# Layer 1's keys, values, contexts and queries of the first batch, made in steps beside the Mamba scans of the second batch

## The chip, the cores and the metric

The kernel runs on one core of one Trainium2 chip. A core has TensorE (PE: matmuls, with weight loads shown apart as PEld), VectorE (DVE), ScalarE (ACT), GpSimd (POOL) and SyncE (SP, which here issues nearly all transfers). The metric is device time in microseconds (us). The kernel before took 5376.03 us, the median of three runs (5373.67 to 5379.39).

## The reference

Four layers work on an image batch `x` of 2 x 256 channels x 48 x 48, all in fp32. In the kernel, L = 48 * 48 = 2304 tokens per batch.

```python
# layer 0: two Mamba branches, forward and backward over the tokens
xs = silu(conv1d(xi)); dt = softplus(...); Bm, Cm = ...
h = exp(d_t * A) * h + (d_t * u_t) * B_t      # 512 channels x 16 states, over 2304 tokens
y = sum_n(h * C_t) + u * D
x = x + (y_f + y_b) @ out_proj_w.T

# layer 1, on v = group-normalized x (32 groups of 8 channels, over a whole image)
q, k, v = relu(t @ Wq + bq) * scale, relu(t @ Wk + bk), t @ Wv + bv
ctx = einsum('bhnd,bhne->bhde', k, v)         # 8 heads of 32, a sum over ALL tokens of a batch
out = einsum('bhnd,bhde->bhne', q, ctx)
img = depthwise_conv3x3(out) + dw_b
t = repbn(t + img @ Wproj + bproj)
t = repbn(t + gelu(t @ Wfc1 + bfc1) @ Wfc2 + bfc2)
x = x + t

# layers 2 and 3: attention, a graph layer with experts (edge_index sorted by target),
# attention again, and a mixture of experts; not touched here
```

Two things matter: the group normalization needs the statistics of a whole image, and the contexts `ctx` need the keys and values of all tokens of that image before its first output can be made. Batch 0's image is finished halfway through layer 0.

## The kernel before, in words

Channels lie on the 128 partitions (256 channels are two halves, `k` or `m`), tokens along the free axis. The residual `E.xres` stays in SBUF. A *piece* is W = 384 tokens; each batch has NCH = 6 pieces, NTB = 18 blocks of 128 tokens.

**Layer 0** (`layer0`) runs 24 *scan steps*, the list `order`: batch 0 forward (steps 0 to 5), batch 0 backward (6 to 11), batch 1 forward (12 to 17), batch 1 backward (18 to 23), one piece each. A scan step (`scan`) handles 4 channel blocks x 16 states: for each, ScalarE makes `hs` (L454, an exponential into one of five PSUM banks), VectorE runs the recurrence (L460 or L463) and, for 40 of 64, the product with `cc` (L468); GpSimd does the other 24 of these products and all of `db` (L437). TensorE sums the products `hc` into `yp` with the identity (`add_state`, L422). Each of the two kinds of `hc` has four buffers. SyncE loads `bb` and `cc` for each group of four states (L432, L434), two buffers each.

A scan step has 32 *slots* (one per two states). The list `beside` holds generators that are advanced as slots go by, each written (steps, number of steps, slot by which to be done): `prepare` for the next scan step, `project_out` for the last piece of a backward step, and either `project_in` (steps 0 to 9) or three steps of `head_products` (steps 10 to 21). In step 13 the statistics of batch 0 are taken beside the scan (`group_stats`: twelve `bn_stats`, then two small matmuls with `gmat` and a square root). While scans run, all products of the beside work go through one PSUM bank, the tag `mm` of pool `ps` (`hold`), so a product waits until the one before it has been read. `head_products` has 12 rounds of three steps: load six blocks `w_eo`; a product `pg` read into `part`; twelve tiny products `pu` read into `ub`.

**Layer 1** (`layer1`), for b = 0 and then 1: group-normalize the batch into `E.xn` (`group_norm`, L597); a loop over 18 blocks makes keys and values `kv` (L611, bias L616, ReLU L617) and sums the contexts `cx` (L619), masked per head with `hmask`; then six pieces go through `image` (queries L633, times contexts L640, written to the padded image `img`), `conv` (18 taps on VectorE, L655 and L659), `project` (L670) and `mlp` (L691 and L710). The image is three pieces ahead. `group_norm(1)`, with the statistics of batch 1, is called after the fourth piece of batch 0. After each piece come lists of the edge sort for layer 2 (`sort_list`, L902 to L925), which nothing in layer 1 reads.

The order in which the program is written is a priority: the framework's planner orders each engine's instructions by it and by its own estimate of when they are ready, so an instruction from later in the text may be put into a gap. The semaphores follow from the data. Each engine then runs its queue strictly in that order.

## Time and profile before

One execution was profiled. It took 5420.46 us, with a span of 5418.6 us from its first to its last instruction; the three timed runs had a median of 5376.03 us.

| stretch of the profile | from, to (us) | what |
|---|---|---|
| start of layer 0 | 0 to 103.9 | first projections, first `prepare` |
| scan steps, batch 0 | 103.9 to 1286.0 | 12 steps of 89.2 to 104.3 us |
| scan steps, batch 1 | 1286.0 to 2431.6 | 12 steps of 89.7 to 102.5 us, the last one 87.9 with the end of layer 0 |
| layer 1 | 2431.6 to 3131.9 | 700.3 us |
| layers 2 and 3, output | 3131.9 to 5418.6 | not touched |

Over the span PE is busy 88%, DVE 65%, ACT 44% and POOL 44%. A busy share counts the time in which an engine has an instruction in it. PE's ends are modelled: back to back, a matmul instruction of 128x384 takes a step of 0.32 us, though it is shown with 0.49 us, since neighbours overlap; one fp32 product is two such instructions. The granted clock is the share of full speed at which TensorE was allowed to run (mean 0.954). In the view of waits, "A <- B" means that an idle time of A's engine ended when B was done.

### The profile page before, as it was taken

The page shows a single profiled execution, that of the slowest core. Times are in us where ns is not written, and L with a number is a line of the kernel's source. Part 1 is how long each engine was busy: PE and PEld are TensorE (multiplying, and loading weights), DVE is VectorE, ACT ScalarE, POOL GpSimd, SP SyncE. Part 2 cuts the span into 40 slices and gives each one's busy share as a digit, 9 for nine tenths or more (in the row PEclk, how much of TensorE's full clock was granted, in tenths as well). Part 3 has the DMA queues.
Part 4 walks back from the last instruction along what each step waited for, and adds up shares of the span by engine and source line. Part 5 has one row for each costly group of instructions (what it writes and reads, how often), then busy time and mean ns, then how long its engine had stood idle before and what let it go on. Part 6 is the DMA issues. An engine that isn't in the chain of part 4 may idle for free. (4 is left out here: it accounts for less than half of the span.)

```text
span 5418.6 us, 47326 instructions
## 1 busy us (share of the span) xinstructions
PE 4773.2 (88%) x15246; PEld 2642.9 (49%) x15246; DVE 3503.3 (65%) x5372; ACT 2370.0 (44%) x4939; POOL 2403.7 (44%) x1308
## 2 busy tenths in 40 slices
PE   7888888888787778879999989999799999999897
PEld 3444444444343344435555555556455455555675
DVE  4999888898999888899996244546534401212343
ACT  5767767666677666642223223422122222222111
POOL 2888888788888888880000000038502100000331
PEclk8999999999899899989999999999898999999899
DMA  4454454444454444431110000111121200000422
GB/s 152 166 177 173 164 178 170 159 162 151 160 174 158 173 166 158 148 137 61 33 45 6 1 16 0 40 29 30 15 72 52 61 7 9 6 9 6 83 83 94
DMA packets 185425, 499.13 MB, mean 92 GB/s; under 512 B 33382, under 2 KB 106474, under 8 KB 184906
## 3 DMA queue, kind: packets, MB, share of 16 engines
q1 hardware_dynamic: 176458, 483.23, 26.1%
q0 software_dynamic: 8704, 12.73, 1.6%
q8 instruction: 124, 2.03, 0.2%
q14 instruction: 139, 1.14, 0.1%
HBM read 422.73 MB, written 73.15 MB: 92 GB/s over the span
## 5 line engine op out<-in xcount | busy, mean ns | idle before, releaser
L422 PE MATMUL yp<-hc,ident 128*128 128x384 f32 x3072 | 1201.7, 523 | 253.2 <-DVE hc L468 210.9
L437 POOL TENSOR_TENSOR db<-dtu,bb 128x1536 f32<-128x1536 f32 x384 | 1329.1, 3462 | 64.6 <-DVE hs L463 21.0
L422 PEld LDWEIGHTS yp<-hc,ident 128*128 128x128 f32 x3072 | 576.2, 199 | 830.2 <-DVE hc L468 408.5
L468 POOL TENSOR_TENSOR hc<-ho,cc 128x384 f32<-128x384 f32 x576 | 584.9, 1023 | 189.9 <-DVE ho L460 82.6
L468 DVE TENSOR_TENSOR hc<-hs,cc 128x384 f32<-128x384 f32 x960 | 496.7, 537 | 57.9 <-PE yp L422 56.6
L454 ACT ACTIVATE hs<-dt,negab 128x384 f32<-128x384 f32 x768 | 435.9, 581 | 93.9 <-DVE hc L468 43.1
L454 ACT ACTIVATE hs<-dt,negaf 128x384 f32<-128x384 f32 x768 | 433.7, 581 | 65.0 <-DVE ho L460 28.8
L463 DVE TENSOR_TENSOR_SCAN hs<-hs,state,db 128x384 f32<-128x384 f32 x400 | 393.8, 1006 | 50.2 <-POOL db L437 23.8
L460 DVE TENSOR_TENSOR_SCAN hs<-hs,state,db 128x384 f32<-128x384 f32 x400 | 395.3, 1007 | 27.4 <-POOL db L437 19.6
L1813 POOL DMA_INDIRECT xe<-xt_d,token x48 | 47.4, 988 | 754.4 <-issue 715.3
L302 PE MATMUL mm<-xw,w_cv 128*128 128x384 f32 x768 | 292.4, 520 | 60.2 <-DVE xres L364 22.0
L1748 PE MATMUL po<-at,xtok 128*128 128x384 f32 x864 | 329.7, 506 | 8.2 <-ACT at L1746 8.1
L953 POOL PARTITION_ALL_REDUCE most<-most x1 | 0.4, 381 | 721.4 <-DVE mx L811 721.4
L1739 PE MATMUL sp<-qT,xn 128*128 128x384 f32 x864 | 317.2, 486 | 0.0
L1746 ACT ACTIVATE at<-sp 128x384 f32<-128x384 f32 x216 | 104.8, 491 | 473.1 <-PE sp L1739 473.0
L1395 PE MATMUL ph<-xn,w 128*128 128x384 f32 x768 | 287.0, 515 | 16.8 <-DMA y_d<-y 5.9
L1399 ACT ACTIVATE hid<-ph,vec 128x384 f32<-128x384 f32 x192 | 110.6, 581 | 337.2 <-PE ph L1395 244.6
L691 PE MATMUL pf<-t,wfc 128*128 128x384 f32 x768 | 255.3, 488 | 0.0
L710 PE MATMUL po<-hid,wfc 128*128 128x384 f32 x768 | 253.6, 486 | 0.0
L470 ACT COPY state<-hs 128x1 f32<-128x1 f32 x800 | 117.7, 155 | 293.6 <-DVE hc L468 291.7
L463 DVE TENSOR_TENSOR_SCAN ho<-hs,state,db 128x384 f32<-128x384 f32 x240 | 238.9, 995 | 10.3 <-ACT hs L454 10.2
L460 DVE TENSOR_TENSOR_SCAN ho<-hs,state,db 128x384 f32<-128x384 f32 x240 | 238.6, 994 | 7.0 <-ACT hs L454 6.6
(442 smaller groups left out, 7970.5 us busy)
## 6 DMA issues: line engine op xcount, KB each, us to landing
bb<-bcd SPq DMA_DIRECT2D x192, 768.0 KB
cc<-bcd SPq DMA_DIRECT2D x192, 768.0 KB
xw<-xi_d SPq DMA_DIRECT2D x24, 774.0 KB
w<-in_m_w SPq DMA_DIRECT2D x16, 1024.0 KB
y_d<-y SPq DMA_DIRECT2D x32, 384.0 KB
ye<-y_d SPq DMA_DIRECT2D x32, 384.0 KB
xi_d<-xz SPq DMA_DIRECT2D x48, 192.0 KB
z_d<-xz SPq DMA_DIRECT2D x48, 192.0 KB
```

The lines of the kernel that those rows point to most:

```text
L302: nc.tensor.matmul(px, lhsT=w_cv[b, s][:, d * 4 + k, :], rhs=xw[:, d, o : o + W], start=k == 0, stop=k == 3,)
L422: nc.tensor.matmul(yp[d], lhsT=E.ident, rhs=hc, start=False, stop=summed[d] == NS)
L437: nc.gpsimd.tensor_tensor(db, bc(dtu[:, d, :], [P, GN, W], 1), bb, ALU.mult)
L454: nc.scalar.activation(hs, dt[:, d, :], AF.Exp, scale=nega[s][:, d * NS + n : d * NS + n + 1])
L460: nc.vector.tensor_tensor_scan(to, hs, db[:, j], init, ALU.mult, ALU.add)
L463: nc.vector.tensor_tensor_scan(to[:, ::-1], hs[:, ::-1], db[:, j, ::-1], init, ALU.mult, ALU.add)
L468: (nc.gpsimd if on_pool else nc.vector).tensor_tensor(hc, to, cc[:, j, :], ALU.mult)
L691: nc.tensor.matmul(pf, lhsT=wfc1[:, k, f * P : (f + 1) * P], rhs=t1[:, k, :], start=k == 0, stop=k == 1,)
L710: nc.tensor.matmul(po[m], lhsT=wfc2[:, f, m * P : (m + 1) * P], rhs=hid[:, i, :], start=f == 0, stop=f == 15,)
L1395: nc.tensor.matmul(ph, lhsT=w1[:, e, k, f * P : (f + 1) * P], rhs=xn[:, k, c * W : (c + 1) * W], start=k == 0, stop=k == 1,)
L1739: nc.tensor.matmul(sp, lhsT=xn[:, k, t0 + i * P : t0 + (i + 1) * P], rhs=qT[:, k, c * W : (c + 1) * W], start=k == 0, stop=k == 1,)
L1748: nc.tensor.matmul(po[m], lhsT=xtok[:, i, m * P : (m + 1) * P], rhs=at, start=i == 0, stop=i == MT - 1,)
```

## The change

Batch 0's part of layer 1 that precedes the convolution moves into layer 0, and batch 1's statistics move too.

- `contexts`, a new generator, is chained behind `head_products`. It loads `Wqkv` into the space of `w_in`, and makes for each piece of batch 0 the normalized tokens (ScalarE), keys and values of three blocks (biases by a matmul of one row) and their sum `cx`; then, for each piece again, the queries and their product with the masked contexts, `qc`, stored to DRAM (`qc_d`). It has 61 steps, which take their SBUF from tiles of `project_in`.
- The chained generators are advanced eight steps in each of the scan steps 10 to 22 (`n_late` = 97 / 13, rounded up), where it was three steps in 10 to 21.
- `piece_stats` takes the two `bn_stats` of each finished piece right behind its `project_out`, for both batches; `group_stats` keeps only the rest. Batch 0's is still in step 13; batch 1's is now at the start of layer 1.
- Layer 1 starts with batch 1: its statistics, its keys and values. Normalizing either batch goes on by pieces between the blocks of that loop. Batch 0's image is filled by `fetch`: a load of `qc` by SyncE, and two copies on GpSimd. Batch 1 keeps its image by matmuls, now called `second`. The loads of `Wfc1` and `Wfc2` come behind the first three `fetch`es.
- `hmask` is built at the start of the program.

```diff
+            self.hmask = const.tile([P, P], F32, name="hmask")
+            same_block(self, wp, self.hmask, 5, 32**-0.5)
...
+def piece_stats(E, b, c):
+    for k in range(2):
+        at = b * L + c * W
+        E.nc.vector.bn_stats(E.st[:, b, k, c, :], E.xres[:, k, at : at + W])
+        yield
...
     for k in range(2):
-        st = wp.tile([P, NCH, 6], F32, tag="st", name="st")
-        for c in range(NCH):
-            nc.vector.bn_stats(st[:, c, :], xb[:, k, c * W : (c + 1) * W])
-            yield
-        nc.vector.bn_aggr(mv[:, k, :], st)
+        nc.vector.bn_aggr(mv[:, k, :], E.st[:, b, k])
...
+    def contexts():
...
+        nc.sync.dma_start(wqkv, p["Wqkv"].rearrange("(k p) m -> p k m", p=P))
+        nc.sync.dma_start(bkv, p["bqkv"][C:].unsqueeze(0))
...
+        def normed(c):
+            xn = up.tile([P, 2, W], F32, tag="pos", name="xn0")
+            for k in range(2):
+                nc.scalar.activation(
+                    xn[:, k, :], E.xres[:, k, c * W : (c + 1) * W], AF.Identity,
+                    bias=off[:, k : k + 1], scale=E.gn[:, 0, 1, k : k + 1],
+                )
+            return xn
+
+        for c in range(NCH):
+            xn = normed(c)
+            yield
...
+            for t in range(3):
+                pk = ps.tile([P, 2 * C], F32, tag="mm", name="pk")
+                for k in range(2):
+                    nc.tensor.matmul(
+                        pk, lhsT=xn[:, k, t * P : (t + 1) * P], rhs=wqkv[:, k, C:],
+                        start=k == 0, stop=False,
+                    )
+                nc.tensor.matmul(pk, lhsT=E.mean_c[0:1, :], rhs=bkv, start=False, stop=True)
+                nc.scalar.activation(kv[t][0], pk[:, :C], AF.Relu)
+                nc.scalar.copy(kv[t][1], pk[:, C:])
+                yield
+            pc = ps.tile([P, C], F32, tag="mm", name="pc")
+            for m in range(2):
+                ms = slice(m * P, (m + 1) * P)
+                for t in range(3):
+                    nc.tensor.matmul(
+                        pc[:, ms], lhsT=kv[t][0][:, ms], rhs=kv[t][1][:, ms], start=t == 0, stop=t == 2
+                    )
+            if c == 0:
+                nc.scalar.copy(cx, pc)
+            else:
+                nc.vector.tensor_tensor(cx, cx, pc, ALU.add)
+            yield
...
+        for c in range(NCH):
+            xn = normed(c)
+            yield
...
+            for m in range(2):
+                pq = hold()
+                for k in range(2):
+                    nc.tensor.matmul(
+                        pq, lhsT=wqkv[:, k, m * P : (m + 1) * P], rhs=xn[:, k, :],
+                        start=k == 0, stop=k == 1,
+                    )
+                nc.scalar.activation(q[:, m, :], pq, AF.Relu, bias=E.v("bq", m, 1))
+                yield
...
+            for m in range(2):
+                pi = hold()
+                nc.tensor.matmul(pi, lhsT=cx[:, m, :], rhs=q[:, m, :], start=True, stop=True)
+                nc.scalar.copy(qc[:, m, :], pi)
+                if m:
+                    nc.sync.dma_start(E.qc_d[:, c], qc)
+                yield
...
-    heads = head_products()
+    heads = chain(head_products(), contexts())
+    n_late = -(-(36 + 1 + 2 * 5 * NCH) // (len(order) - 1 - len(pieces)))
...
-        beside = [(after, 2, 5)] if after else []
+        beside = [(after, 4, 8)] if after else []
...
-        elif i < len(pieces) + 12:
-            beside.append((islice(heads, 3), 3, 32))
+        elif len(pieces) <= i < len(order) - 1:
+            beside.append((islice(heads, n_late), n_late, 32))
         if (b, s, step) == (1, "f", 1):
-            beside.append((group_stats(E, up, lambda: hold()[:, 0:2], 0), 15, 32))
+            beside.append((group_stats(E, up, lambda: hold()[:, 0:2], 0), 3, 20))
         scan(step, beside, *now)
-        after = project_out(b, c, now[4]) if s == "b" else None
+        after = chain(project_out(b, c, now[4]), piece_stats(E, b, c)) if s == "b" else None
...
+    def fetch(c):
+        q = wp.tile([P, 2, W], F32, tag="q", name="q")
+        nc.sync.dma_start(q, E.qc_d[:, c])
+        for m in range(2):
+            nc.gpsimd.tensor_copy(
+                img[:, m, 1 + c * RW : 1 + (c + 1) * RW, 1 : WW + 1],
+                q[:, m].rearrange("p (r w) -> p r w", w=WW),
+            )
+
+    run(group_stats(E, wp, lambda: ps.tile([P, 2], F32, tag="mm", name="pg"), 1))
+    group_norm(1, 0, 1)
+    for c in range(3):
+        fetch(c)
+    wfc1 = big.tile([P, 2, 2048], F32, name="wfc1")
+    nc.sync.dma_start(wfc1, p["Wfc1"].rearrange("(k p) m -> p k m", p=P))
+    wfc2 = big.tile([P, 16, C], F32, name="wfc2")
+    nc.sync.dma_start(wfc2, p["Wfc2"].rearrange("(k p) m -> p k m", p=P))
...
+    for t in range(NTB):
...
+        if t % 3 == 0:
+            if t // 3 + 1 < NCH:
+                group_norm(1, t // 3 + 1, 1)
+            if t >= 6:
+                group_norm(0, t // 3 - 2, 1)
+    group_norm(0, NCH - 2, 2)
...
+        image = second if b else fetch
+        for c in range(3 if b else 0):
             image(c)
...
-            if b + 1 < NB and c == NCH - 3:
-                group_norm(b + 1)
```

## The prediction

> **What bounds the kernel now.** First the page's slices of 135.5 us, to see which engine is full where. The Mamba layer fills the first 18 (to 2431.6 us, when layer 0's last product ends in the timeline), layer 1 the next five (to 3131.9, when layer 2's first transpose starts).
>
> ```profile
> PE   7888888888787778879999989999799999999897
> DVE  4999888898999888899996244546534401212343
> POOL 2888888788888888880000000038502100000331
> ```
>
> In the Mamba layer VectorE, GpSimd and TensorE all stand at 8 or 9 tenths. In layer 1 TensorE is at 9, and so is VectorE for three slices. So I must learn what a piece of work is worth in either place. I cut the Mamba layer at its 24 scan steps (first scan instruction of each) in the view of windows; columns: stretch, length, busy us of PE, PEld, DVE, ACT, POOL, granted clock, DMA share, GB/s.
>
> ```profile
> 289.60:386.10 96.50, 79.57 (x224) 39.48 (x224) 89.49 (x114) 69.46 (x169) 83.16 (x42) 1.00 0.49 168
> 985.40:1089.70 104.30, 87.46 (x249) 44.94 (x248) 91.75 (x120) 71.07 (x164) 81.33 (x42) 0.98 0.49 167
> 1568.40:1660.50 92.10, 75.92 (x212) 36.75 (x212) 86.90 (x112) 63.07 (x157) 82.47 (x42) 0.98 0.48 166
> 2144.90:2247.40 102.50, 86.17 (x227) 43.64 (x226) 86.91 (x117) 65.15 (x154) 81.37 (x42) 0.90 0.42 149
> 2247.40:2343.70 96.30, 78.36 (x208) 39.82 (x207) 85.41 (x114) 64.26 (x153) 81.00 (x41) 0.91 0.41 148
> ```
>
> In order: a forward and a backward step with an input projection beside the scan (`project_in`, 12 steps of beside work), a forward and a backward one with three steps of `head_products`, and a backward one with neither. They are my price list. Layer 1 in four stretches (first keys/values loop; batch 0; second loop; batch 1), same columns:
>
> ```profile
> 2431.60:2484.90 53.30, 45.49 (x153) 24.07 (x152) 52.23 (x110) 9.97 (x23) 4.45 (x2) 0.90 0.38 132
> 2484.90:2789.90 305.00, 294.32 (x904) 172.13 (x905) 289.02 (x565) 87.38 (x140) 0.00 (x0) 0.98 0.12 38
> 2789.90:2850.00 60.10, 56.63 (x185) 30.37 (x183) 55.17 (x110) 14.85 (x32) 0.00 (x0) 0.94 0.11 35
> 2850.00:3131.90 281.90, 281.85 (x872) 165.49 (x873) 131.19 (x221) 81.72 (x129) 0.00 (x0) 1.00 0.01 3
> ```
>
> TensorE works 678 of 700 us. Its waits from 2431 to 3250 us (total, times, longest):
>
> ```profile
> PE pg L149 <- DVE dv L147: 9.8, 1, 9.8
> PE pk L611 <- DMA wproj<-in_Wproj: 6.8, 1, 6.8
> PE cx L619 <- ACT kv L617: 3.7, 3, 3.0
> PE pp L670 <- DVE dw L659: 1.1, 2, 0.7
> ```
>
> VectorE's 95% in batch 0 is largely the edge sort (MAX8 and MATCH_REPLACE8 alone: 88.2 + 86.4 us), for which nothing in layer 1 waits; for the convolution TensorE waits 1.1 us in all. TensorE bounds layer 1.
>
> **What leaves layer 1.** (1) One of two keys/values loops: the second ran from 2789.91 to 2838.83 with 2.58 us of query matmuls inside, so 46.3 us. (2) Batch 0's queries: per piece the timeline steps 2.58 us over eight query matmul instructions and 1.29 over four context ones; six pieces, 23.2 us. (3) The stop at 2690, where batch 1's statistics sit in TensorE's queue between two pieces: 9.8 us, 0.4 of small matmuls, and 1.7 because the next 32 matmuls took 12.16 us at a lower clock where others took 10.48: 11.9. Together 81.4 us, all on the path.
>
> **The new front of layer 1.** Batch 1's keys now come first and need its statistics: after the last `xres` sum (2431.64, 0.55) two bn_stats (0.54), two aggregates (0.30), matmul, copy, three small operations (0.15 each), matmul, square root (0.26), reciprocal (0.16), two normalizations (0.47 each, as L677): some 5 us of instructions, perhaps 8 with the hand-overs. Before, the weights' transfer held TensorE until 2438.43 and the first `kv` came out of VectorE at 2444.95. I take 3 us; the ends are 0 (the transfer covers the chain) and 9.8 (the same chain behind other VectorE work, row L149). The memset of `img` on GpSimd is at the front in both kernels; beside it VectorE's L597 took 5.10 us where the second of the pair took 1.45.
>
> SyncE issues three loads of `qc_d` (393 KB each) ahead of `wfc1` and `wfc2`; the third waits for a GpSimd copy, which waits for the memset (2436.3). The two 2 MB loads then go some 7 us after 2433.2; at the 350 GB/s that the transfer view shows there they take 12 us, and are first wanted after the key loop, near 2485. Free; without that cover, up to 12. GpSimd gets 12 copies of 128x384, about 1 us each (its 128x384 products take 1.02); it is otherwise idle in layer 1 and the image is ready three pieces ahead. The hidden cost is VectorE's: see the rule below.
>
> **What the Mamba layer gains in work.** Beside work is 36 head steps and 61 context steps (1, then 5 for each of 12 pieces), eight per scan step: 13 scan steps (10 to 22) hold 104, so all 97 fit. Every product goes through the one `mm` bank, in TensorE's queue order: behind a product that waits for its bank stand the sums of the scan, behind them the four `hc` buffers, and then VectorE.
>
> *Price of a step.* Against the bare backward step, `project_in` costs 104.3 - 96.3 = 8.0 us for 12 steps. Its VectorE instructions are 7.3 us (0.94, 2.53, 2.69 and two of 0.60, from the forward step), so its 20 matmul pairs and 10 us of ScalarE cost 0.06 us a step: its bank is emptied by ScalarE. The heads cost 102.5 - 96.3 = 6.2 for three steps, 2.07 each, with under 1 us of VectorE work: two of their three drains are VectorE's, behind everything else in its queue; the tile view has TensorE waiting on the drain of `ub` 6.6 us at L359 and 5.1 at L302. Forward there is no bare step: 96.5 with `project_in` against 92.1 with heads is less than the VectorE work between them.
>
> *Contexts.* Keys: 18 steps with three matmul pairs of 128x512 and two ScalarE drains (0.42 and 0.48); 6 sums; 12 queries, 12 contexts, 12 normalizations of 2 x 0.58 on ScalarE. Nearly all drains are ScalarE's, as in `project_in`, but a key step is twice as long a burst. I take 0.4 a step, a fifth of the way from 0.06 to 2.07: 24 us; ends 4 and 116 (33 backward steps at 2.07, 28 forward ones at 1.7, a third of the 5.2 us that VectorE stood idle in a forward step). VectorE gets five sums of 128x256 (0.41, row L783), a mask and small things: 3 us, one to one.
>
> *Heads.* 18 backward and 18 forward steps become 16 and 20: -4 to 0. Closer together, their six loads (786 KB) come every 12 of 32 slots; in the waits of steps 12 to 23 no scan instruction waits for a transfer of theirs. I take +6 for the crowding in steps 10 and 11; ends -4 and +32 (their price doubled there).
>
> *Statistics.* Batch 0's 12 bn_stats only move from step 13 to steps 7 to 12; batch 1's come from layer 1, where they were hidden: 12 x 0.54 = 6.5 us on the bound engine.
>
> *Transfers.* `Wqkv` (768 KB) once, and six stores of `qc`. A store waits on SyncE for a ScalarE copy, and behind it stand the loads of `bb` and `cc`. The eight stores of each `project_in` wait the same way, and at those steps VectorE and GpSimd wait for no `bb` or `cc`: nothing. If that cover were gone, six waits of up to 3.7 us (the longest of an `xz` copy for its product), 22 us. The second mask is built in the first 30 us, where VectorE is busy 8.5: nothing, else 5.
>
> **Sum.** Mamba layer 24 + 3 + 6 + 6.5 = +39.5; layer 1 -81.4 + 3 = -78.4; net -39 of the profiled execution's 5420.5 us (span 5418.6 and 1.9 around it). The median of the three runs, 5376.03, is 0.8% shorter; -39 becomes -38.7, so 5337 us.
>
> **A rule against the change.** The timeline shows VectorE held for about 4 us beside GpSimd's memset, as told. The Trainium skill, "SBUF — State Buffer", section "Who interferes with whom", says that a VectorE instruction with two SBUF inputs and a GpSimd instruction that reads SBUF exclude one another for the whole instruction. By it each of the 12 copies could stop a convolution tap for 1 us: 12 us of VectorE. The sum by the rule would be -27, were VectorE the bound in layer 1; by the rows it stays -39.
>
> **Rivals.**
> - *The one bank (slower).* Context steps cost what head steps cost: 116 + 15.5 - 78.4 = +53, about 5429 us. For it: DVE waits for PE at L468 for 15.9 us over backward steps 19 to 21. Against: `project_in`. It decides from (78.4 - 15.5) / 61 = 1.03 us a step on.
> - *VectorE bounds layer 1.* Then only its share leaves: 18 `kv` sums of 0.68, the bn_stats 6.5, the mask 4.3: 23 us, and 39.5 - 23 = +16, about 5392. For it: 95% busy in batch 0. Against: from 2850 on it is busy under half, since the sort ran ahead.
> - *Steps as free as `project_in`'s.* 4 + 3 - 4 + 6.5 - 81.4 + 3 = -69, about 5308. For it: the clock is 0.98 to 1.00 with `project_in`'s matmuls and 0.90 with the heads', so denser matmuls need not slow the rest.
>
> **Chances.** Forecast (net -55 to -15, 5321 to 5361) 0.62; one bank 0.13; VectorE 0.05; free steps 0.15; between forecast and no change 0.05. Within 0.2% (10.8 us) is about what a measurement of this kernel can tell from no change. Faster: 0.62 + 0.15 and a little of the rest, 0.78; within: 0.07; slower: 0.15. The range reaches from the free steps (5300) to the lower part of the rivals above (5385).
>
> **What the profile after will show.** Right: layer 1 from first key product to layer 2's first transpose some 612 us instead of 693.5; no second key loop, no stop at the statistics; scan steps 14 to 21 within 4 us of before; steps 10 and 11 longer by up to 8. Wrong: steps 14 to 22 longer by 8 or more each with VectorE waiting for `yp` at L468's line; or TensorE idle for 20 us and more at the front or within batch 0.

## The result and the profile after

The changed kernel takes 5328.65 us (median of four runs, 5324.93 to 5331.77), the kernel before 5374.85 us (four runs, 5361.44 to 5379.39). The ratio is 0.9918, with a 95% interval of 0.9899 to 0.9937: faster by 46 us.

The profiled executions are compared by stage, each cut at the first scan instruction, at the end of the last `xres` sum of layer 0, and at layer 2's first transpose. In all the fences of windows below the columns are: stretch, its length, busy us of PE, PEld, DVE, ACT and POOL, granted clock, DMA share, GB/s. First the view of windows of the kernel before (scans, layer 1, layers 2 and 3):

```profile
103.90:2432.20 2328.30, 1912.80 (x5232) 953.42 (x5232) 2098.72 (x2738) 1557.80 (x3583) 1961.36 (x986) 0.95 0.47 162
2432.20:3131.90 699.70, 678.29 (x2112) 392.05 (x2113) 527.04 (x1002) 193.47 (x322) 4.08 (x1) 0.98 0.09 31
3131.90:5418.60 2286.70, 2110.10 (x7731) 1260.74 (x7729) 852.92 (x1595) 567.77 (x953) 430.04 (x312) 0.95 0.13 36
```

The same stretches of the changed kernel:

```profile
101.90:2457.40 2355.50, 1977.31 (x5484) 988.74 (x5484) 2100.45 (x2755) 1591.98 (x3669) 1958.53 (x984) 0.96 0.46 162
2457.40:3086.20 628.80, 612.45 (x1897) 355.40 (x1898) 510.34 (x988) 175.04 (x282) 11.80 (x13) 0.99 0.11 38
3086.20:5323.10 2236.90, 2100.29 (x7731) 1260.51 (x7729) 852.85 (x1595) 567.48 (x953) 436.80 (x312) 0.96 0.14 37
```

TensorE's work was moved, not saved: +64.5 us in the Mamba layer, -65.8 us in layer 1. In layer 1 the stretch shrinks by 70.9 us, more than one to one. In the Mamba layer it grows by 27.2 us, 0.42 us for each us of added TensorE work, while VectorE's busy time grows by only 1.7 us. The balance is -43.7 us, and the medians say -46.2.

The third row is a trap. The two profiled executions differ by 95.5 us, and 49.8 of them lie in layers 2 and 3, where nothing was changed and where every instruction count is the same. A second profile of the kernel before (the first experiment) has 2240.9 us there. That one execution was slow in its last stage, and the forecast was made against it.

The slices of the page after (133 us each) show the same in outline for TensorE and VectorE: 8 to 9 tenths for both in the Mamba layer, 9 for TensorE in layer 1.

```profile
PE   7888888888888888888999989999999999999997
...
DVE  4999898989898888899999344546734411212343
```

The lengths of the scan steps that differ (us; steps 0 to 6 agree within 0.2):

| step | 7 | 8 | 9 | 10 | 11 | 12 | 13 | 14 | 15 | 16 | 17 | 18 | 19 | 20 | 21 | 22 |
|---|---|---|---|---|---|---|---|---|---|---|---|---|---|---|---|---|
| before | 103.0 | 104.3 | 104.3 | 99.2 | 97.1 | 94.2 | 97.0 | 91.2 | 92.0 | 92.1 | 89.7 | 99.5 | 100.9 | 102.3 | 102.5 | 96.3 |
| after | 106.0 | 101.8 | 101.9 | 100.3 | 101.0 | 98.0 | 95.1 | 96.9 | 92.7 | 97.9 | 96.6 | 108.3 | 100.4 | 99.6 | 97.8 | 97.7 |

Steps 7 to 12 now take the statistics of batch 0's pieces and 19 to 23 those of batch 1's, 10 to 14 the heads at eight a step, 14 to 18 the key steps of `contexts`, 18 to 22 its queries. The view of windows of the changed kernel for steps 18 (the last key steps), 19 (queries; 100.9 us with heads before) and 22 (one query step; 96.3 us, and bare, before):

```profile
1864.70:1973.00 108.30, 85.78 (x225) 42.39 (x226) 83.91 (x113) 69.83 (x166) 82.44 (x42) 0.91 0.45 157
1973.00:2073.40 100.40, 84.03 (x229) 42.35 (x228) 86.63 (x116) 69.19 (x164) 82.80 (x42) 0.95 0.45 154
2270.80:2368.50 97.70, 79.84 (x211) 40.11 (x210) 86.45 (x117) 64.91 (x155) 81.39 (x42) 0.91 0.42 150
```

VectorE is busy 84 to 87 us in all three, whatever their length: a longer step is one in which it waits.

Layer 1 of the changed kernel, three of its stretches: the front, the key loop, and the change of batches (about from the first MLP product of batch 0's last piece to that of batch 1's first piece).

```profile
2457.40:2466.30 8.90, 1.15 (x4) 1.00 (x4) 8.45 (x28) 1.61 (x4) 5.44 (x4) 0.61 0.93 309
2466.30:2510.60 44.30, 43.78 (x151) 23.36 (x152) 42.82 (x82) 8.79 (x19) 6.37 (x10) 0.96 0.35 124
...
2741.30:2813.00 71.70, 65.31 (x191) 37.03 (x190) 68.52 (x135) 21.95 (x38) 0.00 (x0) 0.95 0.09 30
```

And what TensorE waited for in it (total, times, longest):

```profile
PE pg L150 <- issue: 5.4, 1, 5.4
PE ln_mean L113 <- DVE ln_half L110: 4.3, 1, 4.3
PE pf L800 <- ACT hid L804: 2.7, 2, 2.0
...
PE pf L800 <- DVE t L783: 0.9, 1, 0.9
```

The 9.8 us stop at the statistics and the 6.8 us for a transfer are gone, as is the second key loop. New are the front (`pg`, 8.9 us from the last `xres` sum to the first key product, where it was 6.2 before) and a group of waits at the change of batches, `ln_mean` above all. Over the change, the distance between the first MLP products of two pieces is 71.7 us (109.5 before, with the second key loop in it); it is 45.2 us within batch 0, and 47.5 for the last pair there. From the first key product to layer 2's first transpose layer 1 takes 619.9 us, where some 612 were forecast and 693.5 were needed before.

### The profile page after: what moved, and what is told of

Its sections match the earlier page's. It is cut to its first block, busy times and chain, and to the rows that moved or that the text cites. A ratio compares the mean times of both kernels' runs of the same rounds, so it can differ in the third digit from the quotient of the medians.

```text
span 5323.1 us, 47473 instructions
## 1 busy us (share of the span) xinstructions
PE 4760.4 (89%) x15282; PEld 2640.7 (50%) x15282; DVE 3489.3 (66%) x5378; ACT 2385.4 (45%) x4985; POOL 2415.8 (45%) x1320
## 5 line engine op out<-in xcount | busy, mean ns | idle before, releaser
L512 PE MATMUL yp<-hc,ident 128*128 128x384 f32 x3072 | 1182.7, 516 | 205.6 <-DVE hc L558 165.2
L558 POOL TENSOR_TENSOR hc<-ho,cc 128x384 f32<-128x384 f32 x576 | 587.4, 1027 | 236.6 <-DVE ho L553 106.0
L544 ACT ACTIVATE hs<-dt,negab 128x384 f32<-128x384 f32 x768 | 435.2, 581 | 94.9 <-DVE hc L558 45.2
L550 DVE TENSOR_TENSOR_SCAN hs<-hs,state,db 128x384 f32<-128x384 f32 x400 | 395.1, 1007 | 34.5 <-POOL db L527 21.5
L311 PE MATMUL mm<-xw,w_cv 128*128 128x384 f32 x768 | 285.8, 514 | 57.0 <-ACT xs L315 18.0
L1854 ACT ACTIVATE at<-sp 128x384 f32<-128x384 f32 x216 | 104.6, 490 | 472.7 <-PE sp L1847 472.6
L553 DVE TENSOR_TENSOR_SCAN ho<-hs,state,db 128x384 f32<-128x384 f32 x240 | 239.0, 996 | 13.8 <-ACT hs L544 13.6
L311 PEld LDWEIGHTS mm<-xw,w_cv 128*128 128x128 f32 x768 | 146.7, 197 | 188.4 <-ACT xs L315 31.4
```

Source lines behind the costliest of these rows:

```text
L311: nc.tensor.matmul(px, lhsT=w_cv[b, s][:, d * 4 + k, :], rhs=xw[:, d, o : o + W], start=k == 0, stop=k == 3,)
L512: nc.tensor.matmul(yp[d], lhsT=E.ident, rhs=hc, start=False, stop=summed[d] == NS)
L544: nc.scalar.activation(hs, dt[:, d, :], AF.Exp, scale=nega[s][:, d * NS + n : d * NS + n + 1])
L550: nc.vector.tensor_tensor_scan(to, hs, db[:, j], init, ALU.mult, ALU.add)
L553: nc.vector.tensor_tensor_scan(to[:, ::-1], hs[:, ::-1], db[:, j, ::-1], init, ALU.mult, ALU.add)
L558: (nc.gpsimd if on_pool else nc.vector).tensor_tensor(hc, to, cc[:, j, :], ALU.mult)
```

## The experiments

Where a run's Mamba layer is given, it is from the first scan instruction to the last `xres` sum: 2355.5 us in the changed kernel, 2328.3 before. The first scan instruction comes at 100.9 to 104.6 us, for reasons outside this study. Layer 1 is from there to layer 2's first transpose: 628.8 us, and 699.7 before.

### The kernel before, once more

No edit.

> The kernel before, unchanged, for a second profile. The profiled execution of before took 5420.5 us, 45 more than the median of the timed runs; its layers 2 and 3 took 2286.7 us (3131.9 to 5418.6), those of the changed kernel 2236.9. If that difference belongs to the one profiled execution: layers 2 and 3 take about 2240 us here, the time is 5361 to 5380, and the Mamba layer (end at 2432.2 us) and layer 1 (699.7 us) are as before within 1 us. If it belongs to the change: 2285 us again, and a time near 5420.

Measured: 5371.05 us. Its Mamba layer takes 2327.8 us and its layer 1 698.5. View of windows, layers 2 and 3:

```profile
3128.30:5369.20 2240.90, 2098.44 (x7731) 1258.51 (x7729) 851.74 (x1595) 568.00 (x953) 436.91 (x312) 0.96 0.14 37
```

The Mamba layer repeats within 0.5 us and layer 1 within 1.3. For the changed kernel the runs below show more: two whose layer 0 is not edited (those of the border and of the sort) have Mamba layers of 2356.1 and 2352.3 us, with step 18 at 108.4 and 106.1 us, while their steps 15 to 17 repeat within 0.1; and layer 1, where it is not edited, takes 628.7 to 632.1 us in seven profiles. So a difference under 4 us of a whole stage can't be read from single profiles, one in a place that repeats can; differences of whole executions cannot.

### What do the contexts cost: the steps without their work

The 61 steps and the six stores stay, the normalizations, products, drains and sums of `contexts` are left out, and each store sends a piece of the residual.

```diff
         for c in range(NCH):
-            xn = normed(c)
-            yield
...
-            for t in range(3):
-                pk = ps.tile([P, 2 * C], F32, tag="mm", name="pk")
...
+            for _ in range(5):
                 yield
```

> The changed kernel without the work of the contexts: the 61 steps stay, but they make no normalization, no product and no drain; only the six stores to the buffer of queries remain, straight from the residual, so batch 0's layer 1 works on wrong numbers. The time of the Mamba layer is what is asked. Theory (the prediction's sum: contexts 24 + 3, heads 6, statistics 6.5): it ends 27 us earlier than in the changed kernel, 2430 instead of 2457.4, and steps 15 to 21 are all shorter than before, since the heads have left them. Rival (the crowded heads and the statistics are the price, contexts are free): it ends at 2450 or later. Layer 1 as in the changed kernel, 628.7 us within 3.

Measured: 5299.49 us. View of windows, the Mamba layer, and then the sum of another answer, over steps 15 to 18 (91.0, 91.3, 87.9 and 103.9 us):

```profile
103.50:2431.50 2328.00, 1912.02 (x5232) 955.28 (x5232) 2104.95 (x2749) 1559.35 (x3584) 1959.45 (x984) 0.95 0.47 164
```

```profile
sum 374.10, PE 288.58 PEld 135.81 DVE 340.20 ACT 252.14 POOL 330.05; mean PE 72.14 PEld 33.95 DVE 85.05 ACT 63.03 POOL 82.51
```

The work of the contexts costs 2355.5 - 2328.0 = 27.5 us, and layer 1 is untouched by it (628.9). Of the 27.5 us, 21.5 lie in steps 15 to 18 (395.6 with the work, 374.1 without), where 15 of the 18 key steps are; the query steps behind them share nearly all of the other 6. Everything else that the change does to the Mamba layer comes in sum to 2328.0 - 2328.3: nothing. Step 18 is long without the contexts too (103.9 us against 99.5 before, where it was to be shorter); that is taken up below.

### What does the denser spacing of the heads cost

The kernel before, with its heads eight a step in steps 10 to 14 instead of three.

```diff
-        elif i < len(pieces) + 12:
-            beside.append((islice(heads, 3), 3, 32))
+        elif len(pieces) <= i < len(order) - 1:
+            beside.append((islice(heads, 8), 8, 32))
```

> The kernel before with one part of the change alone: eight steps of head_products in each of the scan steps 10 to 14 in place of three in 10 to 21; nothing else. It gives the bare steps that the trace of before lacked, forward 15 to 17 and backward 18 to 21. Theory (2.07 us for each head step in a backward scan step, 1 to 1.7 in a forward one, and 6 us for the crowding): steps 10 and 11 are longer by 5 to 10 each, steps 18 to 21 fall to about 96, the forward ones to 88 to 90, and the Mamba layer ends at 2438, 6 us later than before. Rival (the heads cost the same wherever they are): 2432. Second rival (crowded heads cost double): 2460.

Measured: 5373.81 us, Mamba layer 2334.1 us: +6.3 on the second profile of before, +5.8 on the first. The size is as expected, the place is not: steps 10 and 11 grow by 2.6 and 2.8, step 12 by 9.5 and step 14 by 7.6 us, and what the heads leave behind becomes cheaper, but for step 18, which is 103.9 us where some 96 were expected. The view of windows, step 20 of this run, is a bare backward step (102.3 us with three head steps):

```profile
2059.10:2155.30 96.20, 76.88 (x209) 39.21 (x208) 85.41 (x115) 64.67 (x154) 81.27 (x42) 0.93 0.45 157
```

So three head steps do cost some 6 us in a backward step, as the price list had it (4.5 to 6.3 in steps 19 to 21). In the forward steps 15 to 17 their absence gives back 0.9 to 1.7 us a step, 0.4 a head step. By difference to the run before (2328.0 against 2334.1) the moved statistics and whatever else is left cost -6 us, where the prediction had them at +6.5. Step by step the two runs tell more: the one without the contexts' work is 4.7 us longer in steps 19 to 23, where batch 1's statistics are additional, and 11.8 us shorter in steps 7 to 14, to which batch 0's only moved. No run had the statistics alone.

### Is it the engine that empties the bank? (1) Key drains on VectorE

```diff
-                nc.scalar.activation(kv[t][0], pk[:, :C], AF.Relu)
-                nc.scalar.copy(kv[t][1], pk[:, C:])
+                nc.vector.tensor_scalar(kv[t][0], pk[:, :C], 0.0, None, ALU.max)
+                nc.vector.tensor_copy(kv[t][1], pk[:, C:])
```

> The changed kernel with the two drains of each key step moved from ScalarE to VectorE (a maximum with zero and a copy), nothing left out. Theory (a step is cheap because ScalarE empties the bank; behind VectorE's queue it costs what a step of the heads costs): besides the 18 x 0.82 = 15 us of work that VectorE gets, each of the 18 steps pays 1.5 to 2 us of waiting, so the Mamba layer ends 42 to 50 us later than 2457.4. Rival (it does not matter who empties the bank): 15 us later or less, since ScalarE loses as much.

Measured: 5324.76 us, Mamba layer 2351.5 us, 4.0 *shorter* than with ScalarE's drains, though another profile of the unedited layer 0 has 2352.3. View of windows, the sum over steps 15 to 18 (95.3, 98.3, 96.9 and 100.3 us):

```profile
sum 390.80, PE 334.89 PEld 163.17 DVE 343.64 ACT 262.60 POOL 324.63; mean PE 83.72 PEld 40.79 DVE 85.91 ACT 65.65 POOL 81.16
```

Steps 15 to 17 take 290.5 us against 287.3, so the 28 drains of 0.41 us there, moved to VectorE, cost 3 us; step 18 is 8.0 us shorter (5.9 against that other profile), with its longest wait at 7.5 us instead of 10.5 by the view of waits; what else shortened it was not found. The theory that a step behind a VectorE drain is five to thirty times as dear has fallen.

### Is it the engine that empties the bank? (2) Head drains on ScalarE

```diff
-                nc.vector.tensor_tensor(part, part, pg, ALU.add)
+                for k in range(2):
+                    ks = slice(k * C, (k + 1) * C)
+                    nc.scalar.copy(w_eo[k][:, 2 * C :], pg[:, ks])
+                    nc.vector.tensor_tensor(part[:, ks], part[:, ks], w_eo[k][:, 2 * C :], ALU.add)
...
-                nc.vector.tensor_copy(ub, pu[:, 0:2])
+                nc.scalar.copy(ub, pu[:, 0:2])
...
-                nc.vector.tensor_tensor(ub, ub, pu[:, 0:2], ALU.add)
+                ut = up.tile([P, 2], F32, tag="ut", name="ut")
+                nc.scalar.copy(ut, pu[:, 0:2])
+                nc.vector.tensor_tensor(ub, ub, ut, ALU.add)
```

> The two drains of each head round that are VectorE's (pg into part, pu into ub) become ScalarE copies into SBUF, which VectorE then sums from there: the bank no longer waits for VectorE's queue. The prediction's theory (a backward head step costs 2.07 us because VectorE empties its bank): 16 backward steps at 0.1 to 0.4 us, so steps 10 and 11 together 25 to 32 us shorter, both at 90 to 93 us less than... no lower than the bare 96.2, so in fact 192 to 193 in sum instead of 201.3, and steps 12 and 13 2 to 4 us shorter. The rival (it is not the engine that drains, but the products and transfers themselves): steps 10 to 13 within 3 us of 394.4 in sum, or longer by the added ScalarE copies.

Measured: 5342.55 us, Mamba layer 2369.6, 14.1 us *longer*; steps 10 to 13 sum to 409.7 us instead of 394.5. What VectorE waited for in steps 11 and 12 of the changed kernel, and then of this run (total, times, longest):

```profile
DVE hc L558 <- PE yp L512: 6.1, 10, 0.9
DVE ub L412 <- PE pu L406: 3.8, 3, 1.9
...
DVE part L399 <- PE pg L392: 1.5, 1, 1.5
```

```profile
DVE hc L564 <- PE yp L518: 11.6, 12, 2.1
...
DVE ub L420 <- ACT ut L419: 1.0, 1, 1.0
DVE part L403 <- ACT w_eo L402: 0.9, 1, 0.9
```

The waits of VectorE for the heads' products are gone, 5.3 us in two steps, 1.9 us of waits for ScalarE's copies stand in their place, and the waits for the scan's sums have grown by 5.5. The edit isn't pure: VectorE's sums now read a third part of the `w_eo` tiles, so the next loads into those wait for them. But the theory expected the heads to become nearly free, and nothing of that is to be seen.

### Is it TensorE's time? Key steps without their bias product

The one-row bias product is left out; steps, drains and hand-overs stay.

```diff
                         pk, lhsT=xn[:, k, t * P : (t + 1) * P], rhs=wqkv[:, k, C:],
-                        start=k == 0, stop=False,
+                        start=k == 0, stop=k == 1,
                     )
-                nc.tensor.matmul(pk, lhsT=E.mean_c[0:1, :], rhs=bkv, start=False, stop=True)
```

> The bias product of one row is left out of the 18 key steps (the keys and values in the Mamba layer lack their bias, so the output differs); all steps, drains and hand-overs stay. It takes 18 x 0.86 = 15.5 us of TensorE's 77 us of context work away. If TensorE's time sets the price of a step, steps 15 to 18 become shorter by a share of that: 26/77 of it, 5 us in sum, and up to 15.5 if every us of it stood in the scan's way. If the number of steps and their hand-overs (bank, drains) sets it, within 1.5 us of the changed kernel in sum (392 us in steps 15 to 18).

Measured: 5326.81 us (one execution, whose layers 2 and 3 are 11 us longer than in the changed kernel's profile), Mamba layer 2342.8, 12.7 us shorter. View of windows, the sum over steps 15 to 18 of the changed kernel, then of this run:

```profile
sum 395.60, PE 332.44 PEld 161.28 DVE 335.36 ACT 270.73 POOL 325.63; mean PE 83.11 PEld 40.32 DVE 83.84 ACT 67.68 POOL 81.41
```

```profile
sum 381.80, PE 319.44 PEld 158.45 DVE 335.93 ACT 270.14 POOL 325.63; mean PE 79.86 PEld 39.61 DVE 83.98 ACT 67.54 POOL 81.41
```

TensorE is busy 13.0 us less, VectorE, ScalarE and GpSimd stay within 0.6, and the four steps are 13.8 us shorter, although TensorE is idle for 63 of the 395.6 us. Of the 13.8, 4.2 lie in step 18, which differs by 2.2 between profiles of one and the same layer 0; steps 15 to 17, which repeat, gain 9.7 for 14 bias products of 0.86 us, 12.0. At the margin, then, a us of TensorE's time in a key step costs the scan some 0.8 to 1 us. Where it is lost is seen in VectorE's waits in steps 16 and 17, in the changed kernel and then in this run (total, times, longest):

```profile
DVE hc L558 <- PE yp L512: 9.3, 7, 3.1
DVE hs L550 <- ACT hs L544: 4.2, 8, 1.1
DVE ho L550 <- ACT hs L544: 3.8, 4, 2.1
```

```profile
DVE hc L557 <- PE yp L511: 3.3, 7, 0.7
```

VectorE's next product waits for a buffer of `hc`, which comes free when TensorE has summed the product in it, and these sums stand behind the key products in TensorE's queue. In the run without the contexts' work this wait is not there. But a shorter key product also leaves the one bank sooner, so this run alone does not tell TensorE's time from the time for which the bank is held; the next one bears on that.

The average over all the contexts is only 0.42. A reading that fits both: the scan hides a burst of matmuls up to some length, and pays for what is longer. A key step is one burst of six instructions, 18 x 0.86 = 15.5 us for a third of it, so 2.6 us long; the 18 key steps, in scan steps 14 to 18, cost 22.0 / 18 = 1.2 us each if the short steps between them cost nothing, so 1.4 us of a burst would be hidden. The bursts of the query steps and of `project_in` are four instructions of 0.32 us, 1.3 us long, and cost about 0.2 and 0.06 us a step. The product `pg` of the heads is a burst as long as a key step's, once in three head steps: they cost 1.3 us in a forward step, as this reading would have it, but some 6 in a backward one, which it leaves open. Most key steps lie in forward scan steps and the queries in backward ones, and the length of the burst was not varied in any other run, so this reading is a theory.

### Does the one bank set the price? Two banks

```diff
-    psh = ctx.enter_context(tc.tile_pool(name="l0ps_h", bufs=5, space=PSUM))
-    ps = ctx.enter_context(tc.tile_pool(name="l0ps_s", bufs=1, space=PSUM))
+    psh = ctx.enter_context(tc.tile_pool(name="l0ps_h", bufs=4, space=PSUM))
+    ps = ctx.enter_context(tc.tile_pool(name="l0ps_s", bufs=2, space=PSUM))
```

> The changed kernel with a second bank for the products of the beside work, taken from the five of hs, which keep four. Theory that is left after the last runs (contexts cost 26 us since TensorE's sums stand behind products that wait for the one bank, whoever drains it): steps 14 to 18 fall by 10 to 20 us in all, since a product finds a free bank. Rival (with four banks ScalarE cannot run ahead, and VectorE waits for hs): every scan step of the layer gets longer, the early ones with project_in too, by 2 to 8 us each, 50 us and more in all. Second rival (the price is the work of ScalarE and TensorE itself): no change within 5 us.

Measured: 5320.45 us, Mamba layer 2342.8, 12.7 us shorter, of which steps 15 to 17 (279.8 instead of 287.3) give 7.5: step 15 is 1.2 longer, steps 16 and 17 are 3.8 and 4.8 shorter. Steps 14 to 18, where 10 to 20 us were expected, are 8.2 shorter. VectorE's longest waits in steps 16 and 17 with two banks; for `yp` there is none any more:

```profile
DVE hs L550 <- ACT hs L544: 6.4, 7, 2.9
DVE ho L550 <- ACT hs L544: 3.5, 3, 2.5
```

TensorE is as busy in these two steps as in the changed kernel (166.15 us against 166.17), and they take 185.9 us instead of 194.5; without the bias product, with 7.4 us less of TensorE's time, they took 186.4. So it is not TensorE's time alone that makes the wait for `yp`: with the same time and a second bank it is gone, and `hs`, now at four banks, is waited for 1.9 us longer. The single bank is a part of the price of the key steps: 7.5 of the 17.1 us that the contexts cost in steps 15 to 17 (287.3 - 270.2), as far as one `hs` bank less makes no difference there, and not the 50 us of the rival. The forward steps of batch 0 change by -4.1 to +2.5 each. One edit changes two pools here, so the rest of the 12.7 us is not assigned.

### The long first backward step: `yf` later

Step 18 begins the backward scan of batch 1. What VectorE waits for in it, in the changed kernel:

```profile
DVE hc L558 <- PE yp L512: 15.4, 7, 10.5
```

SyncE's queue there, in the timeline (start, us, line, operation):

```profile
1869.25 0.42 SPq L576 DMA_DIRECT2D yf_d<-y  x1
1878.52 0.32 SPq L522 DMA_DIRECT2D bb<-bcd  x1
1878.89 0.43 SPq L505 DMA_DIRECT2D yf<-yf_d  x1
```

The forward sum of the piece just scanned goes out at 1869.25 and is wanted back as `yf`; its load stands behind a load of `bb`, which leaves only at 1878.52. It lands 6.2 us after its issue, at 1885.11. The product of `yf` (L537) starts at 1887.71 in the timeline, right behind beside products (L311) that began at 1883.71, and it stands in TensorE's queue ahead of the sums of the scan. The kernel before has the same wait (8.4 us by the view of waits), and so has the run without contexts (9.7). The edit moves that product, for the first two channel blocks, from the front to between the seventh and the eighth sum (the count goes up before it is compared, so it is one sum earlier than the expectation says):

```diff
         def add_state(d, hc):
+            if not fwd and d < 2 and summed[d] == NS // 2:
+                nc.tensor.matmul(yp[d], lhsT=E.ident, rhs=yf[:, d, :], start=False, stop=False)
...
-                    if not fwd:
+                    if not fwd and d >= 2:
                         nc.tensor.matmul(
                             yp[d], lhsT=E.ident, rhs=yf[:, d, :], start=False, stop=False
                         )
```

> The changed kernel with the product that adds the forward branch's yf moved, for the first two channel blocks of a backward step, from before the scan's sums to between the eighth and the ninth. In scan step 18 (108.3 us, the longest) VectorE waits 10.5 us at one place for yp: yf was stored at the end of step 17, its load stands in SyncE's queue behind a load of bb that waits for its buffer until 1878.5, and TensorE's sums stand behind yf's product at 1887.7. Theory (that round trip, not the context steps, is what makes step 18 long): step 18 falls to 97 to 100, step 6 (100.8, the same place in batch 0) by 2 to 4, the other backward steps stay within 2. Rival (step 18 is long because it holds eight crowded steps): 105 or more.

Measured: 5324.09 us, Mamba layer 2345.1 us, 10.4 shorter. Step 18 goes from 108.3 to 96.8 us and step 6, its counterpart in batch 0, from 100.8 to 97.5; the 10.5 us wait is gone (the longest wait for `yp` in step 18 is 0.7). So the place of this product in the queue makes the wait. How much of it was the round trip of `yf`, and how much the products ahead, no run separates. Steps 8 and 9 become 4 us longer each, where the other backward steps were to stay within 2, for a reason that was not found.

### The front of layer 1: only the border of `img`

VectorE's instructions at the front, in the timeline of the changed kernel; beside them GpSimd's memset of `img` runs from 2457.24 to 2461.51:

```profile
2457.34 4.24 DVE L1001 CAST lo_row<-iota 128x128 f32<-128x128 int32 x1
2457.48 4.11 DVE L138 BATCH_NORM_STATS2 st<-xres 128x6 f32<-128x384 f32 x1
```

Both end at 2461.6, with the memset; so do the aggregation (3.64 us) and a normalization (3.62) behind them. One is held, the others queue behind it, and batch 1's last statistics are among them. Only the border of `img` needs zeros, since the rest is written later:

```diff
-    nc.gpsimd.memset(img, 0.0)
+    nc.gpsimd.memset(img[:, :, 0 : HH + 2 : HH + 1, :], 0.0)
+    nc.gpsimd.memset(img[:, :, :, 0 : WW + 2 : WW + 1], 0.0)
```

> The changed kernel with the memset of img cut to its border (two memsets, of the first and last row and the first and last column, in place of one of 5000 elements a partition). At the front of layer 1 GpSimd's memset runs from 2457.2 to 2461.5 and VectorE's cast, bn_stats and aggregates that were started beside it end together at 2461.5. Theory (the memset holds VectorE, and batch 1's statistics are now behind it): TensorE's first key product comes 5 us after the last sum of the Mamba layer instead of 8.9, and layer 1 takes 3 to 4 us less than 628.7. Rival (the weights' transfer or the chain of small operations sets the start): no more than 1 us.

Measured: layer 1 624.5 us, 4.3 shorter; from the last `xres` sum to the first key product 5.1 us instead of 8.9. The same instructions in this run's timeline:

```profile
2456.94 0.24 DVE L1002 CAST lo_row<-iota 128x128 f32<-128x128 int32 x1
2457.07 0.55 DVE L138 BATCH_NORM_STATS2 st<-xres 128x6 f32<-128x384 f32 x1
```

The whole execution, a single one, was 5333.41 us; the gain is smaller than the spread of layers 2 and 3 between executions, and is read from the stage alone.

### The change of batches: the sort held back

The lists of the edge sort of batch 1's half are queued only behind the last tap of batch 1's first convolution.

```diff
+        first_conv = taps[-1]
...
             while n_list * NB * NCH < edges.NL * (b * NCH + c + 1):
-                edges.sort_list(E, gp, n_list)
+                if b:
+                    with tc.issue_after(first_conv.ins):
+                        edges.sort_list(E, gp, n_list)
+                else:
+                    edges.sort_list(E, gp, n_list)
                 n_list += 1
```

> The changed kernel with the sort lists that belong to batch 1 (the last eight) kept behind the first convolution of batch 1 in VectorE's queue; nothing left out. In the changed kernel the first MLP product of batch 1 comes 71.7 us after that of batch 0's last piece, where its matmuls need 60.7, and TensorE waits there 4.3 us for a sum of the layer norm, 2.0 for a hidden piece and runs at half clock. Theory (VectorE is late there because sort instructions stand between): that distance falls to 62 to 66, the 0.9 and 2.0 us stops in batch 0's last pieces go, and layer 1 takes 5 to 9 us less than 628.7. Rival (the convolution of batch 1 cannot start before its image, whatever the sort does): 70 us or more, layer 1 within 2 us.

Measured: 5315.96 us, layer 1 617.2 us, 11.6 shorter. The longest waits of TensorE in its layer 1, and then (view of windows) its change of batches:

```profile
PE pg L150 <- issue: 5.4, 1, 5.4
PE pk L709 <- DVE xn L680: 1.5, 1, 1.5
```

```profile
2735.10:2800.00 64.90, 64.69 (x199) 37.14 (x198) 29.90 (x50) 24.29 (x39) 0.00 (x0) 1.00 0.00 1
```

The waits for `ln_half`, `hid` and `t` are all gone, 7.9 us in sum. The distance of first MLP products over the change falls from 71.7 to 62.6 us and the one before it from 47.5 to 45.2: 11.4 of the 11.6. It is more than the waits themselves, since the granted clock over that stretch also goes from 0.95 to 1.00 (5% of 71.7 us is 3.6). So VectorE does bound the changed layer 1 in one place: the sort, which nothing there reads, ran ahead into the queue between a layer norm and the next image.

### Together

Border, held-back sort and later `yf` in one kernel; and the same with two banks.

> Border instead of whole memset, held-back sort lists and the later yf product together, in the changed kernel. They lie in three different places, so the first theory (each gain is that of its own wait) says that they add: Mamba layer 11 us shorter than in the changed kernel (its end near 2446), layer 1 4 + 11 us shorter (628.7 to some 613), together -27 us, about 5302 and a ratio of 0.9865 to the kernel before. The rival (the profiled single looks owe part of their gains to the noise of one execution, some 5 us a look) says -10 to -15, about 5316.

> The same with two banks for the beside products (five banks of hs become four). If the bank's gain lies in the context steps and the yf gain in steps 6 and 18, they add: another -10 us, about 5292, with steps 14 to 17 some 4 us shorter in sum and the forward steps 2 to 4 of batch 0 1 us longer each. If both only shift the same slack of VectorE's scan, the second brings nothing: 5302.

Measured: the three together 5306.43 us (four runs, 5299.94 to 5311.77), ratio to the kernel before 0.9878 (0.9859 to 0.9896); the four together 5295.47 us (5287.69 to 5300.59), ratio 0.9852 (0.9833 to 0.9870). The Mamba layer in the view of windows, first with three, then with four (layer 1 takes 614.6 and 614.9 us):

```profile
101.40:2446.20 2344.80, 1974.20 (x5484) 986.07 (x5484) 2099.31 (x2755) 1595.59 (x3669) 1955.90 (x984) 0.96 0.45 163
```

```profile
101.80:2441.60 2339.80, 1984.45 (x5476) 995.09 (x5476) 2120.70 (x2752) 1601.92 (x3671) 1961.75 (x985) 0.95 0.45 163
```

The three add up: -10.7 us in the Mamba layer (alone: -10.4) and -14.2 in layer 1 (alone: -4.3 and -11.6), 24.9 by stages, 22 by the medians. The second bank, 12.7 us alone, adds only 5.0 to that by stages: alone it seems to gain in part where the later `yf` gains. Steps 14 to 17, which were to gain some 4 us by it, gain 2.2. The medians differ by 11.0 us, but the intervals overlap, so whether four are better than three stays unclear. Both beat the kernel before, and the four beat the changed kernel by their intervals (0.9833 to 0.9870 against 0.9899 to 0.9937).

## Why the prediction was right, and where it was wrong

The forecast was 5337 us, a gain of 39; measured 5328.65, a gain of 46. The sum, term by term:

| term | predicted | measured | by |
|---|---|---|---|
| contexts, with VectorE's sums | 24 + 3 | 27.5 | the run without their work |
| crowding of the heads | 6 | 5.8 to 6.3 | heads eight a step in the kernel before |
| statistics in the Mamba layer, and the rest | 6.5 | -6 | difference of those two runs |
| Mamba layer | +39.5 | +27.2 | the profiles |
| front of layer 1 | 3 | 2.7 | 8.9 against 6.2 us |
| the rest of layer 1 | -81.4 | -73.6 | -70.9 - 2.7 |
| net | -39 | -43.7 | the profiles |

That the net is off by less than 5 us is in part luck: the Mamba layer was put 12.3 us too high and the gain of layer 1 7.5 us too high, and the two errors work against each other.

**The contexts.** The amount was right and the path too; what the price was scaled by was not, so that 27 us came out is in part luck. The path, "behind a product that waits for its bank stand the sums of the scan, behind them the four `hc` buffers, and then VectorE", is the one that the key steps show: 9.3 us of waiting for `yp` in steps 16 and 17, and none with a second bank. But "I take 0.4 a step, a fifth of the way from 0.06 to 2.07" rested on "its bank is emptied by ScalarE". Neither run that swapped the draining engine bore that out: VectorE drains made the key steps 3 us dearer in three steps, not 40, and ScalarE drains made the heads dearer instead of free. The two rows compared, `project_in` and the heads, differ in more than the drain. A key step gets cheaper by a shorter product (7.4 us of TensorE's time less in steps 16 and 17, 8.1 us gained) as well as by a second bank (8.6 us gained there); both shorten the same wait, and how the price is divided between them was not measured. The 0.4 is also no price of any step: it is a mean of key pieces at some 0.7 a step and query pieces at 0.2.

**Crowding.** Right in sum, wrong in place. Steps 10 and 11 were to be up to 8 us longer and became 1.1 and 3.9; steps 12 and 14 took the rest in the run that shows it alone. The same goes for "steps 14 to 21 within 4 us of before": 14, 16, 17 and 18 are 5.7 to 8.8 us longer, 21 is 4.7 shorter. The text's own sign for the bank rival, every step from 14 to 22 longer by 8 with VectorE waiting for `yp`, was seen in part: step 18 is 8.8 longer, but there the sums stand behind the product of `yf`, and steps 16 and 17 are 5.8 and 6.9 longer, with 9.3 us of waiting for `yp`.

**Statistics.** This term was furthest off, some 12 us: in place of "6.5 us on the bound engine" the layer got 6 us shorter by the difference of two runs, though VectorE's busy time is 6 us more without the contexts than before (2104.95 against 2098.72). The 6.5 itself is not what failed: where batch 1's statistics are additional, steps 19 to 23, the layer is 4.7 us longer. What failed is the nothing put on "Batch 0's 12 bn_stats only move from step 13 to steps 7 to 12": steps 7 to 14 are 11.8 us shorter. One reading is that twelve `bn_stats` crowded beside one step had cost more than their time, and that, spread over the pieces, they fill waits. But the change also advances `project_out` by other slots there (`(after, 4, 8)` for `(after, 2, 5)`), no run had either alone, and the cause stays open.

**Layer 1.** The parts that leave were sized well, and the front had the right size (2.7 against 3). Its reason was another: the text has "some 5 us of instructions, perhaps 8 with the hand-overs", and the border run takes 5.1 us for the whole chain, hand-overs included; what made it 8.9 was the memset, which the text names beside it without a price. With the sort held back the rest would have been -73.6 - 11.6 = -85.2, a little more than the -81.4 forecast. The step that failed is that VectorE's 95% is "largely the edge sort", "for which nothing in layer 1 waits; for the convolution TensorE waits 1.1 us in all". It was true of the kernel before and not of the one after: take 70 us of TensorE's time out of a stretch in which VectorE is at 95%, and the second engine is the limit somewhere. The rival "VectorE bounds layer 1" was wrong as a whole, and right for 11 us.

**The rule against the change.** The Trainium skill, "SBUF — State Buffer", section "Who interferes with whom", would have let each of the 12 GpSimd copies stop a convolution tap. The trace agrees in kind and not in size. The taps and the copies of the changed kernel, in the view of the tile `img` (ns, shortest/median/longest):

```profile
L768 DVE SCALAR_TENSOR_TENSOR dw<-img,vec,dw x192: 591/609/856, 2477.7 to 2945.9; 128x384 f32<-128x384 f32 x192
L690 POOL COPY img<-q x12: 505/631/930, 2465.0 to 2485.4; 128x384 f32<-128x384 f32 x12
```

In the kernel before, no tap takes more than 620 ns. Six of the twelve copies run beside the first taps; five taps there take 0.85 us instead of 0.61, 1.2 us in all, and the copies beside them 0.59 to 0.93 instead of 0.51. TensorE waits for none of it: its list has no wait for `dw`. So the 12 us that the rule was priced at came to 1.2; a copy was put at 1 us and takes 0.67. For the memset beside VectorE's cast the same section, which counts casts among the instructions that can contend with GpSimd, agrees: 4.24 us against 0.24.

**The scale.** The forecast was worked out against an execution of 5420.5 us, of which some 46 in layers 2 and 3 belonged to that execution alone. Scaling -39 by 0.8% was harmless only because the change doesn't touch that stage.

## What to carry to other kernels

Moving work from a stage that one engine bounds into one where that engine is idle a fifth of the time pays, but not at the rate of the idle share: look at what stands behind a single uninterrupted piece of the moved work, in the queue and for its bank, and price that. Here the long pieces cost some 1.2 us each and the short ones 0.2 or less, and the long ones became cheaper by shorter products as well as by a second bank. After the bound of a stage is lowered, look again at the engine that was next to it, and hold back what it does for later stages. Compare profiles stage by stage, with a second profile of the kernel before, before a difference between executions is taken for one between kernels.

## What was not expected of the hardware

- VectorE with 36 more instructions of 0.41 us (14.8 us of work in four and a half scan steps, 9.5 us more of busy time) and ScalarE with as many less: the three full steps grew by only 3 us, and a fourth shrank by 8.
- Instructions behind a held one are shown with the whole time of the hold: a `bn_stats` of 0.55 us shows 4.11, an aggregation of 0.30 shows 3.64. A mean of such a group says nothing of the instruction.
- The store of a tile and its load back as `yf` took 15.9 us from the store's issue (1869.25) to the landing (1885.11), more than half of it behind another load in SyncE's queue; the product came another 2.6 us later.
- Identical code in layers 2 and 3 took 2236.9, 2240.9 and 2286.7 us in three executions, with TensorE's busy time at 2100.3, 2098.4 and 2110.1 us. In the eleven other profiles it took 2237 to 2250 us.
